# A decoder layer with routed experts: sends in fours, last additions on VectorE, longer runs in DRAM

## The chip, the cores and the metric

The kernel runs on one core of one Trainium2 chip. The core has five engines with instruction queues of their own: TensorE (PE, with its weight loads shown as PEld), VectorE (DVE), ScalarE (ACT), GpSimd (POOL) and SyncE (SP), and 16 DMA engines that they share. The metric is the device time of one execution in microseconds (us), as a median over runs. A separate execution is recorded by the hardware profiler, and all rows below come from that one.

## The reference

One pre-norm decoder layer in fp32 over 1024 tokens of width D = 256 (16 sequences of 64):

```python
x = x + attention(layernorm(x))          # 16 heads of 128, weights = codes * scales
x = x + cross_attention(layernorm(x), ctx)   # 16 heads, rope, low-rank keys and values
x = x + experts(layernorm(x))

def experts(x):
    scores = softmax(x @ Wg.T)                         # 16 experts in 4 groups
    # the 2 best groups, then the 4 best experts within them
    h = silu(x @ W1[e].T) * (x @ W3[e].T)              # inner width 176
    y = sum over the token's 4 experts of scores[e] * (h @ W2[e].T)
    z = (silu(x @ Ws1.T) * (x @ Ws3.T)) @ Ws2.T        # shared expert
    return y + z
```

## The kernel before, in words

Matrix products run on pairs of fp32r numbers: `parts_of` (L111) splits a value into a high part, written by ACT (L112), and a low part, written by DVE (L113), and `three` (L107) and `matmuls` (L104) multiply high by high, high by low and low by high. The tokens are held as eight tiles `x[i]` of 128 rows, in two halves of four tiles.

The cross attention goes through its 16 heads in quads of four. `quad_steps` (L403) loads a quad's weights from DRAM: `Wq` and `Wo` as 128 partitions with four pieces of 1024 bytes each, `w_kc_q` with four of 768, `w_kc_kv` with four of 256.

The experts follow. For each half, `choose` works out a target row for every token and each of its four choices k. `send` (L837) scatters the token's row, 272 floats or 1088 bytes, by indirect DMAs from POOL's queue into the DRAM buffer `xd`: 16 sends in each half, four for each k. Every expert but the last has 384 slots in `xd`. The last expert, and the tokens for which an expert's slots don't suffice, are computed densely. Then the loop over `e` takes the experts through a pipeline of stages:

- `expert_inputs(e)` (L1251) loads the expert's slots `xr` (408 KB, L1255, on SP's queue, behind the sends of choices 0 to e), PE transposes them in six pieces (L1265), ACT and DVE split them into `xs`.
- `expert_weights(e)` loads the raw weights `w` (640 KB, L277, on SP's queue, into one of two buffers) and splits them: ACT copies (L278), DVE and DVE or POOL subtract (L283).
- `expert_hidden` multiplies 18 times, ACT applies Silu in two steps (L1283, L1286), DVE multiplies (L1284, L1287), and the result is split into `hp`.
- `send_outputs` (L1291) multiplies by the second weights, copies the results to `y` (L1299, on ACT, one of three on DVE) and scatters them by three indirect DMAs from POOL's queue (L1304) to the rows of `yd` that belong to a token and its choice.

The loop computes the hidden layer of expert e-1 ahead of the slots of expert e where e is 1 or 2, and behind them otherwise:

```python
for e in range(E + 1):
    if e in (1, 2):
        hs[e - 1] = expert_hidden(ws[e - 1], xs[e - 1][0], SLOTS)
    ...
    if 0 <= e - 1 < E - 1 and e > 2:
        hs[e - 1] = expert_hidden(ws[e - 1], xs[e - 1][0], SLOTS)
```

After experts 11 to 14, `load_outputs(k)` (L1314) loads the outputs of one choice for all tokens, in four loads of 256 KB on SP's queue (L1320) into a pool of nine `got` buffers, each behind all sends of outputs that it may read. At the end `add_outputs` (L1327) adds each output, times the token's weight for it, to `x`. For two of three tiles that is one DVE instruction (L1334), for the third a scaling on ACT (L1331) and an addition on POOL (L1332). The dense part of the last expert for the second half lies between: `dense_hidden`, and `dense_output`, whose results `add_last` adds on DVE (L952). Eight DMAs store `x` (L1392), on the queues of SP and ACT in turn.

The order of instructions on each engine is fixed when the program is built: a scheduler works on estimated times of each instruction, and `issue_after` pins some of them behind others. A change of the program's text can thus move instructions that it doesn't name. Waits on semaphores are derived from buffers and from dependencies that the program declares; `side_by_side` declares that two sends do not depend on each other, and `behind` declares that a load depends on a list of sends.

Of the kernel before, what the change touches and what calls it, by code (L numbers as in the profile page):

```python
# [71 lines left out]
def decoder_layer(ctx: ExitStack, tc: tile.TileContext, a: dict, out: bass.AP):  # L72
# [167 lines left out]

    yd = dram.tile([(E - 1) * SLOTS + TOPK * NT, D], F32, tag="yd", name="yd")

    def side_by_side(sent, others):

        for other in others:
            tc.declare_no_dep(sent, other, reason="each writes rows of its own")
        others.append(sent)

    def behind(read, writes):
# [65 lines left out]
    with ExitStack() as attn:  # L315
# [87 lines left out]
        def quad_steps(qd, weights, pool):  # L403


            hs = slice(4 * qd, 4 * qd + 4)
            wq = raw_tile("wq", [128, 4, D])
            nc.sync.dma_start(
                out=wq,
                in_=a["Wq"][512 * qd : 512 * qd + 512, :].rearrange("(h k) d -> k h d", k=128),  # L410
            )
            wkq = raw_tile("wkq", [128, 4, DCQ])
            nc.sync.dma_start(out=wkq, in_=a["w_kc_q"][hs].rearrange("h k q -> k h q"))
            wqr = raw_tile("wqr", [R, 4, DCQ])
            nc.sync.dma_start(out=wqr, in_=a["W_qrT"][:, hs, :])
            wkr = raw_tile("wkr", [R, 4, DC])
            nc.sync.dma_start(out=wkr, in_=a["W_krT"][:, hs, :])
            wkv = raw_tile("wkv", [128, 4, DC])
            nc.sync.dma_start(out=wkv, in_=a["w_kc_kv"][hs].rearrange("h k d -> k h d"))
            wot = raw_tile("wot", [128, 4, D])  # L420
            quad_loads.append(
                nc.sync.dma_start(
                    out=wot,
                    in_=a["Wo"][512 * qd : 512 * qd + 512, :].rearrange(
                        "(h k) o -> k h o", k=128
                    ),
                ).ins
            )
            w_s = pool.tile([128, 3, 2, 2, DC], F32, tag="w_s", name="w_s")
            nc.gpsimd.memset(w_s, 0.0)  # L430
            yield
            w_q = [
                pool.tile([128, 2, 2, 4 * HQ], F32R, tag=f"w_q{n}", name=f"w_q{n}")
                for n in range(2)
            ]
            for h in range(4):
                ps = mm_tile(cols=2 * DCQ)
                for c in range(2):
                    nc.tensor.matmul(  # L439
                        ps[:, c * DCQ : (c + 1) * DCQ],  # L440
                        lhsT=wq[:, h, c * 128 : (c + 1) * 128],
                        rhs=wkq[:, h, :],
                        start=True,
                        stop=True,
                    )
                cols = slice(h * HQ, (h + 1) * HQ)
                parts_of(
                    ps.rearrange("p (c t j) -> p c t j", c=2, t=2),
                    w_q[0][:, :, :, cols],
                    w_q[1][:, :, :, cols],  # L450
                )
                if h % 2 == 1:
                    yield
            for tiles in ((0, 1), (2,)):
                ps = mm_tile().rearrange("p (t b n d) -> p t b n d", t=2, b=2, n=2)
                for t, row, n, blk, h, j in PIECES:
                    if t not in tiles:
                        continue
                    rows = slice(row, row + n)
                    for ab in range(2):  # L460
                        nc.tensor.matmul(  # L461
                            ps[rows, t % 2, blk, ab, :],
                            lhsT=wqr[:, h, ab * HQ + j : ab * HQ + j + n],
                            rhs=wkr[:, h, :],
                            start=True,
                            stop=True,
                        )
                for t, row, n, blk, h, j in PIECES:
                    if t in tiles:
# [15 lines left out]
            parts_of(ps, w_o[0], w_o[1])  # L485
            weights[qd].append(w_o)
            yield
# [348 lines left out]

        def send(half, choices=range(TOPK), waits=()):  # L837

            to = targets[half]
            for k in choices:  # L840
                for i in range(4):
                    sent = nc.gpsimd.indirect_dma_start(
                        out=xd[: TOPK * NT + (E - 1 - k) * SLOTS],
                        out_offset=bass.IndirectOffsetOnAxis(ap=to[:, k, i : i + 1], axis=0),
                        in_=rows[half][i // 2][:, i % 2, :],
                        in_offset=None,
                    ).ins
                    side_by_side(sent, sent_rows)
                    sent_for[k].append(sent)
                    behind(sent, waits)  # L850

# [399 lines left out]
    def expert_inputs(e):  # L1251

        t = fx.tile([128, SLOTS // 128, ROW], F32, tag="xr", name="xr", bufs=3)
        first = TOPK * NT + (E - 2 - e) * SLOTS
        load = nc.sync.dma_start(  # L1255
            out=t, in_=xd[first : first + SLOTS].rearrange("(b p) d -> p b d", p=128)
        ).ins
        for k in range(min(TOPK, e + 1)):
            behind(load, sent_for[k])
        to = fx.tile([128, SLOTS // 128], U32, tag="to", name="to", bufs=8)  # L1260
        parts = [fx.tile([128, 2, SLOTS], F32R, tag=f"xs{n}", name=f"xs{n}") for n in range(2)]
        for c in range(2):
            ps = at_tile([128, 512])[:, :SLOTS]
            for b in range(SLOTS // 128):
                nc.tensor.transpose(  # L1265
                    ps[:, b * 128 : (b + 1) * 128], t[:, b, c * 128 : (c + 1) * 128], ident
                )
            lows.append(parts_of(ps, parts[0][:, c, :], parts[1][:, c, :]))
        with tc.issue_after(lows[-1]):
            nc.vector.tensor_copy(to, t[:, :, D + e])  # L1270
        return parts, to
# [41 lines left out]

    def load_outputs(k):  # L1314

        tiles = []
        for n in range(NI // 2):
            t = fy.tile([128, 2, D], F32, tag="got", name="got", bufs=9)
            first = (E - 1) * SLOTS + (TOPK - 1 - k) * NT + n * 256
            got = nc.sync.dma_start(  # L1320
                out=t, in_=yd[first : first + 256].rearrange("(i p) d -> p i d", p=128)
            ).ins
            behind(got, returned)
            tiles.append(t)
        return tiles

    def add_outputs(k, got, cw):  # L1327
        for i in range(NI):
            y, w = got[i // 2][:, i % 2], cw[i // 4][:, k, i % 4 : i % 4 + 1]
            if i % 3 == 2:  # L1330
                nc.scalar.activation(y, y, AF.Copy, scale=w)  # L1331
                nc.gpsimd.tensor_tensor(x[i], x[i], y, ALU.add)  # L1332
            else:
                nc.vector.scalar_tensor_tensor(x[i], y, w, x[i], ALU.mult, ALU.add)  # L1334

    def dense_hidden(w, half, n):
        return expert_hidden(w, [p[:, :, n * 256 : n * 256 + 256] for p in normed[half]], 256)
# [13 lines left out]
    with tc.issue_after(lows[-1]), tc.issue_after(silus[-1]):  # L1351
        ws[0] = expert_weights(a["W123"][0], nc.vector)
    for e in range(E + 1):
        if e in (1, 2):

            low = lows[-1]
            hs[e - 1] = expert_hidden(ws[e - 1], xs[e - 1][0], SLOTS)
        if e < E - 1:
            low = lows[-1]
            with tc.issue_after(up_done[0] if e in (1, 2) else low):  # L1360
                xs[e] = expert_inputs(e)
            if e >= 1:
                with tc.issue_after(low), tc.issue_after(silus[-1]):
# [1 line left out]
        if e == 1:  # L1365
            with tc.issue_after(gated[0]), tc.issue_after(silus[-1]):
                routed.append(weights_of_choices(1))
        if 0 <= e - 1 < E - 1 and e > 2:
            hs[e - 1] = expert_hidden(ws[e - 1], xs[e - 1][0], SLOTS)
        if e - 2 >= 0:  # L1370
            if e == E:
# [9 lines left out]
    with ExitStack() as behind_last:  # L1381
        for ins in (*last, gated[0]):
            behind_last.enter_context(tc.issue_after(ins))
        cw = [r[0] for r in routed]
        add_outputs(0, got[0], cw)
        dense_output(w_last, h_p, 1, 0, add_last)
        add_outputs(1, got[1], cw)
        dense_output(w_last, dense_hidden(w_last, 1, 1), 1, 1, add_last)
        for k in range(2, TOPK):
            add_outputs(k, got[k], cw)  # L1390
    for i in range(NI):
        (nc.sync if i % 2 == 0 else nc.scalar).dma_start(  # L1392
# [123 lines left out]
```

## Time and profile before

| | |
|---|---|
| median of three runs | 570.32 us (569.85 to 570.35) |
| profiled execution | 577.4 us |
| its span | 575.5 us |
| mean granted PE clock | 0.978 of full speed |
| DMA | 70.83 MB in 56294 packets |
| entry into the experts | first slots loaded from 446.5 us on |
| last outputs stored | from 566.8 us on |

The profiled execution is 7.1 us above the median of the three runs. The busy shares of the page are averages over the span; the stages have different limits, so a stretch is read from its own windows and its own part of the timeline. In a timeline row the columns are the start, the duration, the engine, the line and operation, output and inputs, and in brackets the idle time before and what ended it. Several like instructions in a row are one line with a count.

### The profile page before, as it was taken

The page shows a single profiled execution, that of the slowest core. Times are in us where ns is not written, and L with a number is a line of the kernel's source. Part 1 is how long each engine was busy: PE and PEld are TensorE (multiplying, and loading weights), DVE is VectorE, ACT ScalarE, POOL GpSimd, SP SyncE. Part 2 cuts the span into 40 slices and gives each one's busy share as a digit, 9 for nine tenths or more (in the row PEclk, how much of TensorE's full clock was granted, in tenths as well). Part 3 has the DMA queues.
Part 4 walks back from the last instruction along what each step waited for, and adds up shares of the span by engine and source line. Part 5 has one row for each costly group of instructions (what it writes and reads, how often), then busy time and mean ns, then how long its engine had stood idle before and what let it go on. Part 6 is the DMA issues. An engine that isn't in the chain of part 4 may idle for free.

```text
span 575.5 us, 10603 instructions
## 1 busy us (share of the span) xinstructions
PE 540.3 (94%) x4013; PEld 446.7 (78%) x4013; DVE 400.2 (70%) x879; ACT 279.3 (49%) x524; POOL 230.6 (40%) x213
## 2 busy tenths in 40 slices
PE   7999999999999989999999999999999779999962
PEld 5889898888989876757778577685787669999951
DVE  6355566644655788848577586889777479999866
ACT  4677557575574431230432323152525187777551
POOL 4260500101001005426243444632544717888862
PEclk9999999999999999999999999999999789999995
DMA  8564431823200599482020000000511658777384
GB/s 227 145 166 146 111 109 39 227 86 112 75 1 1 167 250 308 111 239 52 2 70 1 8 1 1 0 31 0 188 50 68 202 169 285 240 245 238 122 279 152
DMA packets 56294, 70.83 MB, mean 123 GB/s; under 512 B 13872, under 2 KB 42768, under 8 KB 56240
## 3 DMA queue, kind: packets, MB, share of 16 engines
q1 hardware_dynamic: 51408, 58.71, 34.5%
q0 software_dynamic: 3696, 10.36, 4.7%
q10 hardware_dynamic: 1136, 1.05, 0.6%
q8 instruction: 33, 0.54, 0.4%
q14 instruction: 21, 0.17, 0.1%
HBM read 48.61 MB, written 21.86 MB: 122 GB/s over the span
## 4 chain that ended last, share of the span: by engine, by line
PE 81%; DVE 7%; issue 4%; DMA 3%; ACT 3%; POOL 1%; SPq 1%; DVEq 0%; ACTq 0%; POOLq 0%
PE mm L104 47%; PE mm L1005 7%; PE av L590 5%; PE av L104 5%; PE at L573 4%; PE at L343 3%; PE at L1028 2%; PE av L1041 2%; PE at L1265 2%; PE mm L439 2%; DMA bqkv<-in_bqkv 1%; PE mm L461 1%; DMA got<-yd 1%; DVE x L1334 1%; POOL roped L990 1%
## 5 line engine op out<-in xcount | busy, mean ns | idle before, releaser
L990 POOL TENSOR_TENSOR roped<-rt,rt 128x512 f32<-128x512 f32 x48 | 62.6, 1325 | 83.4 <-DVE rt L984 80.5
L984 DVE TENSOR_TENSOR rt<-mm,rope_q 128x512 f32<-128x512 f32 x96 | 61.4, 685 | 24.3 <-PE mm L104 23.6
L104 PE MATMUL mm<-xn,w_q 128*128 128x512 f32 x288 | 73.9, 403 | 0.5 <-ACT xn L222 0.5
L104 PEld LDWEIGHTS mm<-xn,w_q 128*128 128x128 f32 x288 | 52.2, 188 | 14.0 <-issue 1.8
L104 PE MATMUL mm<-xs,w 128*128 128x384 f32 x270 | 55.3, 354 | 7.0 <-ACT xs L112 5.8
L1304 POOL DMA_INDIRECT yd<-y,to x45 | 47.9, 1064 | 27.6 <-ACT y L1299 13.1
L104 PEld LDWEIGHTS mm<-xs,w 128*128 128x128 f32 x270 | 48.4, 198 | 9.0 <-ACT xs L112 6.6
L327 ACT ACTIVATE p<-p 128x512 f32<-128x512 f32 x32 | 20.1, 629 | 62.3 <-DVE p L326 62.3
L324 DVE TENSOR_REDUCE sm_m<-at 128x8 f32<-128x512 f32 x32 | 21.8, 680 | 37.1 <-PE at L573 36.2
L1005 PE MATMUL mm<-roped,w_s 128*64 128x512 f32 x192 | 46.4, 602 | 0.7 <-POOL roped L990 0.7
L522 POOL TENSOR_TENSOR wv<-code,scale 128x512 fp32r<-128x512 f32 x7 | 9.5, 1360 | 88.2 <-DMA scale<-in_scales 58.7
L613 DVE TENSOR_TENSOR x<-mm,x 128x256 f32<-128x256 f32 x64 | 26.0, 419 | 23.9 <-PE mm L104 21.9
L104 PE MATMUL mm<-wo,o 128*128 128x256 f32 x256 | 39.6, 295 | 0.0
L104 PE MATMUL av<-w,hp 128*128 128x256 f32 x225 | 35.2, 290 | 0.7 <-ACT y L1299 0.7
L104 PE MATMUL mm<-xn,wq 128*128 128x512 f32 x128 | 34.6, 405 | 0.7 <-ACT xn L222 0.5
L104 PE MATMUL mm<-wv,xn 128*128 128x256 f32 x256 | 35.2, 289 | 0.0
L104 PE MATMUL mm<-xn,wk 128*128 128x512 f32 x128 | 34.9, 404 | 0.0
L590 PE MATMUL av<-pt,v 128*128 128x128 f32 x256 | 34.5, 277 | 0.0
L104 PEld LDWEIGHTS mm<-wo,o 128*128 128x128 f32 x256 | 32.9, 190 | 1.5 <-issue 0.4
L590 PEld LDWEIGHTS av<-pt,v 128*128 128x128 f32 x256 | 32.0, 191 | 1.2
L104 PEld LDWEIGHTS mm<-wv,xn 128*128 128x128 f32 x256 | 31.8, 189 | 0.9
L104 PEld LDWEIGHTS av<-w,hp 128*128 128x128 f32 x225 | 30.6, 190 | 1.9 <-ACT y L1299 1.2
(216 smaller groups left out, 1145.8 us busy)
## 6 DMA issues: line engine op xcount, KB each, us to landing
w<-in_W SPq DMA_DIRECT2D x15, 640.0 KB
code<-in_codes SPq DMA_DIRECT2D x32, 256.0 KB
scale<-in_scales SPq DMA_DIRECT2D x32, 256.0 KB
xr<-xd SPq DMA_DIRECT2D x15, 408.0 KB
xd<-zeros SPq DMA_DIRECT2D x8, 720.0 KB
yd<-zeros SPq DMA_DIRECT2D x8, 512.0 KB
got<-yd SPq DMA_DIRECT2D x16, 256.0 KB
wq<-in_Wq SPq DMA_DIRECT2D x4, 512.0 KB
```

The lines of the kernel that those rows point to most:

```text
L104: m = nc.tensor.matmul(ps, lhsT=l, rhs=r, start=(n == 0), stop=(n == len(pairs) - 1))
L324: nc.vector.tensor_reduce(m, sc, AX.X, ALU.max)
L327: exps.append(nc.scalar.activation(p, p, AF.Exp, scale=scale).ins)
L343: last = nc.tensor.transpose(ps[:, 2 * n : 2 * n + 2, :].rearrange("p a q -> p (a q)"), pn[:, 2 * n : 2 * n + 2, :].rearrange("p a k -> p ...
L439: nc.tensor.matmul(ps[:, c * DCQ : (c + 1) * DCQ], lhsT=wq[:, h, c * 128 : (c + 1) * 128], rhs=wkq[:, h, :], start=True, stop=True,)
L573: nc.tensor.matmul(sc[par * 64 : par * 64 + 64, 2 * g + pp, :], lhsT=qk[0][:, b * S : (b + 1) * S], rhs=qk[1][:, b * S : (b + 1) * S], sta ...
L590: nc.tensor.matmul(av[:, k * 128 : (k + 1) * 128], lhsT=v[:, i, k0 : k0 + HD], rhs=pt[:, i].rearrange("p a q -> p (a q)"), start=True, sto ...
L613: nc.vector.tensor_tensor(x[i], ps, x[i], ALU.add)
L984: nc.vector.tensor_tensor(mt, ps3, rope_table(t, 2 * ab + k), ALU.mult)
L990: nc.gpsimd.tensor_tensor(r.rearrange("p (b s) -> p b s", s=S), one, two, op)
L1005: nc.tensor.matmul(ps[h // 2][(h % 2) * 64 : (h % 2) * 64 + 64], lhsT=w_s[:, t, blk, ab, :], rhs=roped[2 * t + ab], start=first[h], stop=l ...
L1304: sent = nc.gpsimd.indirect_dma_start(out=yd[: (E - 1) * SLOTS + min(TOPK, E - 1 - e) * NT], out_offset=bass.IndirectOffsetOnAxis(ap=to[:, ...
```

## The change

Seven things are changed.

1. In `send`, for the second half, the four sends of choices 1, 2 and 3 each wait until the last send before them has landed.
2. The slots `xr` are loaded with a partition's three rows side by side in DRAM (3264 bytes in one run, before three of 1088).
3. `load_outputs` takes two rows of `yd` side by side for a partition (2048 bytes, before two of 1024), and `row_of`, by which the outputs are scattered, is permuted to match. For the last choice the four tiles lie in the two raw-weight buffers, and two of the loads go to ACT's queue.
4. `add_outputs` makes all 32 additions on DVE.
5. At the end, the first dense output of the last expert comes ahead of the additions of choice 0, the second hidden layer and output ahead of the additions of choice 1.
6. At e = 3 too, the hidden layer of the expert before comes ahead of the slots.
7. The weights of the cross attention lie in DRAM by quads, so that a partition's piece is one run of 4096, 3072, 1024 and 4096 bytes.

In the built program, the order of instructions on every engine is the same up to the entry into the experts. There, SP's loads stand as xr 0, W 2, xr 1, xr 2, W 3, xr 3, where they stood as xr 0, xr 1, W 2, xr 2, xr 3, W 3.

```diff
-    def side_by_side(sent, others):
+    def side_by_side(sent, others, landed=()):
         for other in others:
-            tc.declare_no_dep(sent, other, reason="each writes rows of its own")
+            if other not in landed:
+                tc.declare_no_dep(sent, other, reason="each writes rows of its own")
         others.append(sent)
...
             wq = raw_tile("wq", [128, 4, D])
-            nc.sync.dma_start(
-                out=wq,
-                in_=a["Wq"][512 * qd : 512 * qd + 512, :].rearrange("(h k) d -> k h d", k=128),
-            )
+            nc.sync.dma_start(out=wq, in_=a["Wq"][qd])
...
             for k in choices:
+                landed = sent_rows[-1:] if half and k else ()
                 for i in range(4):
...
-                    side_by_side(sent, sent_rows)
+                    side_by_side(sent, sent_rows, landed)
...
-            out=t, in_=xd[first : first + SLOTS].rearrange("(b p) d -> p b d", p=128)
+            out=t, in_=xd[first : first + SLOTS].rearrange("(p b) d -> p b d", p=128)
...
-        tiles = []
-        for n in range(NI // 2):
-            t = fy.tile([128, 2, D], F32, tag="got", name="got", bufs=9)
+        if k == TOPK - 1:
+            tiles = [
+                t[:, n * 2 * D : (n + 1) * 2 * D].rearrange("p (i d) -> p i d", i=2)
+                for t in (fw.tile([128, W_COLS], F32, tag="w123", name="got_last") for _ in range(2))
+                for n in range(2)
+            ]
+        else:
+            tiles = [
+                fy.tile([128, 2, D], F32, tag="got", name="got", bufs=9) for _ in range(NI // 2)
+            ]
+        for n, t in enumerate(tiles):
             first = (E - 1) * SLOTS + (TOPK - 1 - k) * NT + n * 256
-            got = nc.sync.dma_start(
-                out=t, in_=yd[first : first + 256].rearrange("(i p) d -> p i d", p=128)
+            got = (nc.scalar if k == TOPK - 1 and n % 2 else nc.sync).dma_start(
+                out=t, in_=yd[first : first + 256].rearrange("(p i) d -> p i d", p=128)
             ).ins
...
-            if i % 3 == 2:
-                nc.scalar.activation(y, y, AF.Copy, scale=w)
-                nc.gpsimd.tensor_tensor(x[i], x[i], y, ALU.add)
-            else:
-                nc.vector.scalar_tensor_tensor(x[i], y, w, x[i], ALU.mult, ALU.add)
+            nc.vector.scalar_tensor_tensor(x[i], y, w, x[i], ALU.mult, ALU.add)
...
-        if e in (1, 2):
+        if e in (1, 2, 3):
...
-            with tc.issue_after(up_done[0] if e in (1, 2) else low):
+            with tc.issue_after(up_done[0] if e in (1, 2, 3) else low):
...
-        if 0 <= e - 1 < E - 1 and e > 2:
+        if 0 <= e - 1 < E - 1 and e > 3:
...
+        dense_output(w_last, h_p, 1, 0, add_last)
         add_outputs(0, got[0], cw)
-        dense_output(w_last, h_p, 1, 0, add_last)
-        add_outputs(1, got[1], cw)
         dense_output(w_last, dense_hidden(w_last, 1, 1), 1, 1, add_last)
-        for k in range(2, TOPK):
+        for k in range(1, TOPK):
             add_outputs(k, got[k], cw)
...
+    def quads(w):
+        return w.reshape(NQ, NH // NQ, HD, -1).transpose(0, 2, 1, 3)
+
+    arrays["Wq"] = quads(v[xa + "Wq"])
...
-    arrays["row_of"] = (
-        (E - 1) * SLOTS + TOPK * NT + np.arange(NT).reshape(NI, 128).T
-    ).astype(np.float32)
+    pairs = np.arange(NT).reshape(NI // 2, 128, 2).transpose(1, 0, 2).reshape(128, NI)
+    arrays["row_of"] = ((E - 1) * SLOTS + TOPK * NT + pairs).astype(np.float32)
```

More of the change, by code (lines that the diff above doesn't have):

```diff
@@ L407, in quad_steps @@
             wq = raw_tile("wq", [128, 4, D])
-            nc.sync.dma_start(
-                out=wq,
-                in_=a["Wq"][512 * qd : 512 * qd + 512, :].rearrange("(h k) d -> k h d", k=128),
-            )
+            nc.sync.dma_start(out=wq, in_=a["Wq"][qd])
             wkq = raw_tile("wkq", [128, 4, DCQ])
-            nc.sync.dma_start(out=wkq, in_=a["w_kc_q"][hs].rearrange("h k q -> k h q"))
+            nc.sync.dma_start(out=wkq, in_=a["w_kc_q"][qd])
             wqr = raw_tile("wqr", [R, 4, DCQ])
@@ L418, in quad_steps @@
             wkv = raw_tile("wkv", [128, 4, DC])
-            nc.sync.dma_start(out=wkv, in_=a["w_kc_kv"][hs].rearrange("h k d -> k h d"))
+            nc.sync.dma_start(out=wkv, in_=a["w_kc_kv"][qd])
             wot = raw_tile("wot", [128, 4, D])
             quad_loads.append(
[L422 to L427, printed above, removed]
+                nc.sync.dma_start(out=wot, in_=a["Wo"][qd]).ins
             )
@@ L1314, in load_outputs @@
     def load_outputs(k):
-        tiles = []
-        for n in range(NI // 2):
-            t = fy.tile([128, 2, D], F32, tag="got", name="got", bufs=9)
+        if k == TOPK - 1:
[9 more added lines that the diff above has]
+        for n, t in enumerate(tiles):
             first = (E - 1) * SLOTS + (TOPK - 1 - k) * NT + n * 256
-            got = nc.sync.dma_start(
-                out=t, in_=yd[first : first + 256].rearrange("(i p) d -> p i d", p=128)
+            got = (nc.scalar if k == TOPK - 1 and n % 2 else nc.sync).dma_start(
+                out=t, in_=yd[first : first + 256].rearrange("(p i) d -> p i d", p=128)
             ).ins
             behind(got, returned)
-            tiles.append(t)
         return tiles
@@ L1468 @@
     arrays["bo"] = v[sa + "bo"]
-    arrays["Wq"] = v[xa + "Wq"]
-    arrays["w_kc_q"] = v[xa + "w_kc_q"]
-    arrays["w_kc_kv"] = v[xa + "w_kc_kv"]
+    def quads(w):
+        return w.reshape(NQ, NH // NQ, HD, -1).transpose(0, 2, 1, 3)
+    arrays["Wq"] = quads(v[xa + "Wq"])
+    arrays["w_kc_q"] = quads(v[xa + "w_kc_q"])
+    arrays["w_kc_kv"] = quads(v[xa + "w_kc_kv"])
     arrays["W_qrT"] = v[xa + "W_qr"].transpose(2, 0, 1)
     arrays["W_krT"] = v[xa + "W_kr"].transpose(2, 0, 1)
-    arrays["Wo"] = v[xa + "Wo"].T
+    arrays["Wo"] = quads(v[xa + "Wo"].T)
     arrays["W123"] = _expert_weights(*(v[ff + n] for n in ("W1", "W3", "W2")))
```

## The prediction

> **What bounds the kernel now.** I read the page first, then the waits of PE, then PE's windows and timeline around the entry into the experts, and last the timeline of the end.
>
> ```profile
> PE 540.3 (94%) x4013; PEld 446.7 (78%) x4013; DVE 400.2 (70%) x879; ACT 279.3 (49%) x524; POOL 230.6 (40%) x213
> ...
> PE 81%; DVE 7%; issue 4%; DMA 3%; ACT 3%; POOL 1%; SPq 1%; DVEq 0%; ACTq 0%; POOLq 0%
> ```
>
> PE is busy for 94% of the 575.5-us span, and 81% of the chain that ended last is PE. A change gains only where PE waits, or in the last stretch, where PE has run out of work. What PE waits for:
>
> ```profile
> PE av L104 <- DVE x L952: 5.8, 2, 4.2
> PE mm L104 <- ACT xs L112: 5.8, 3, 3.2
> ```
>
> These two are the largest of 21 lines (total, times, longest), and none of the 21 names a DMA. The first lies in the last 15 us. The second is the entry into the experts. PE's timeline there, with idle time and releaser in brackets:
>
> ```profile
> 450.68 1.13 PE L104 MATMUL mm<-ws,sh 96*128 96x256 f32 x4 [1.65 <-issue]
> ...
> 454.54 4.82 PE L104 MATMUL mm<-xs,w 128*128 128x384 f32 x18 [1.45 <-ACT xs L112]
> 459.19 0.82 PE L1265 MATMUL at<-ident,xr 128*128 128x128 f32 x6
> 463.24 0.79 PE L104 MATMUL mm<-xs,w 128*128 128x384 f32 x3 [3.23 <-ACT xs L112]
> ...
> 471.41 0.80 PE L104 MATMUL mm<-xs,w 128*128 128x384 f32 x3 [1.10 <-ACT xs L112]
> 472.48 1.08 PE L104 MATMUL av<-w,hp 128*128 128x256 f32 x7 [0.27 <-ACT y L1299]
> 473.56 0.55 PE L1265 MATMUL at<-ident,xr 128*128 128x128 f32 x3
> ```
>
> PE waits at 463.24 and at 471.41 for experts 1 and 2, the two where the loop computes the previous hidden layer ahead of the transposes. From expert 3 (transposes at 473.56 and 475.64) it waits no more. The windows (width, then busy time of PE, PEld, DVE, ACT, POOL, granted clock, DMA share, GB/s):
>
> ```profile
> 450.00:452.00 2.00, 1.32 (x6) 1.32 (x7) 2.00 (x4) 0.00 (x0) 1.85 (x1) 0.70 0.23 81
> 452.00:454.00 2.00, 1.09 (x6) 0.69 (x4) 1.71 (x6) 0.00 (x0) 1.39 (x3) 0.50 0.43 122
> ...
> 480.00:490.00 10.00, 10.00 (x74) 10.00 (x73) 9.18 (x17) 8.40 (x18) 6.63 (x7) 1.00 0.83 277
> 490.00:500.00 10.00, 9.97 (x69) 9.77 (x68) 9.09 (x18) 6.96 (x17) 7.93 (x7) 1.00 0.66 214
> ```
>
> From 472.5 to 550 PE is full (10.00 or 9.63 of 10). Time lost at expert 3 is therefore lost at the end.
>
> The end, from the timeline, is a chain of additions by DVE:
>
> ```profile
> 552.59 3.65 DVE L1334 SCALAR_TENSOR_TENSOR x<-got,cw,x 128x256 f32<-128x256 f32 x9
> 557.09 2.08 POOL L1332 TENSOR_TENSOR x<-x,got 128x256 f32<-128x256 f32 x3
> 558.62 0.85 DVE L1334 SCALAR_TENSOR_TENSOR x<-got,cw,x 128x256 f32<-128x256 f32 x1 [2.38 <-DMA got<-yd]
> ...
> 566.12 0.51 ACT L1331 ACTIVATE got<-got,cw 128x256 f32<-128x256 f32 x1 [1.00 <-DMA got<-yd]
> ...
> 569.50 1.66 DVE L1334 SCALAR_TENSOR_TENSOR x<-got,cw,x 128x256 f32<-128x256 f32 x4
> ```
>
> DVE starts the additions at 552.59 and ends at 571.16. The outputs are then stored and the span ends at 575.5.
>
> **The change part by part.** The sum is made against the profiled execution: 577.4 us, of which 575.5 are the span. It lies 7.1 us above the median of the three runs (570.32), and I carry differences over to the median unchanged.
>
> *Weights of the cross attention as quads.* Sixteen loads (L408 to L427) keep place and bytes and get longer runs. No line of PE's waits names a DMA and nobody is listed as waiting for wq: 0. If that cover went, a shorter load would still not be later. Both bounds are near 0.
>
> *Loop order at e = 3.* Hidden layer 2 (18 matmuls, about 3.4 us at full clock) moves ahead of the transposes of xr 3. The instruction order of the two kernels shows PE then runs as at e = 2: hidden matmuls, six transposes, output matmuls, hidden matmuls of the next expert. ACT's order becomes two Silus, the raw-weight copy of L278, first xs part, hp, second xs part, y. So the row for e = 2 is the price, and it is 1.10 + 0.27 us of idle plus about 0.25 between the pieces, 1.6. Built up by hand: hidden 2 has 15 matmuls left at 473.56, 0.19 each, and ends at 476.4, transposes at 477.2, seven output matmuls at 478.05. ACT ends its second Silu at 477.1, its 1.26-us copy at 478.4 and the first xs part at 478.9: PE waits 0.9. Three matmuls take it to 479.5. The next output matmuls wait for y, behind hp 0.5, xs 0.5 and y 0.37, until 480.35: 0.8. Together 1.7. The bounds are 0 (the copy comes early enough and PE finds other work in its queue) and 2.2 (DVE's 0.96-us L283 gets ahead of the xs parts). Nothing below 0, because before has no wait there. Each 10-us window behind it has at most 0.37 us of idle, so hardly any is made good. Taken: +1.7.
>
> *The clock behind that gap.* In the rows above, 1.65 us of idle ended at 450.68 and the granted clock fell to 0.70 and then 0.50; the 18 matmuls at 454.54 took 4.82 us there instead of 3.4. The Trainium skill, "TensorE: Matmul & The Clock Gate", section "HAM oscillation — how this bites in real kernels", asks that PE have no idle gap over about 3.4 us; by that rule gaps of 0.9 and 0.8 cost nothing and the sum for this part is +1.7. By the trace a gap of half that length can be followed by half clock, and one more hidden layer at half clock costs 1.4: +3.1. The gap at 471.41 (1.10) was followed by 1.00, and it is the nearer in size. I weigh 1.4 by somewhat under one half: +0.6.
>
> *Sends in fours.* Three waits are added on POOL (before k = 1, 2 and 3 of half 1), each for the landing of the last send of the four before. Queued behind each are only later sends, until the first send of outputs at 472.70, before which POOL already sits idle for 11.50 us. A send takes 0.96 us at a pitch of 1.27 and the wait for its landing is bounded by xr 0, which waits for the first four sends: it leaves at 446.53, 2.0 behind the fourth send's end at 444.52. Three gates cost up to 2.0 each, 6 us for k = 3, which would end by 467 instead of 461.2. Who waits is the loads of xr 1, 2 and 3 on SP. On SP, W2 and W3 also change places with xr 1 and xr 3: W2 ahead of xr 1 (it waits for DVE's L283 until 452.1, so xr 1 leaves near 452.9 instead of 452.36 and shares the engines with 640 KB), xr 3 ahead of W3. xr 1 landing 1.5 later than its 455.7 is still ahead of its transposes at 459.19. xr 2 leaves near 460, as now (459.83), for transposes at 469.02. xr 3 leaves by 469 instead of 463.50 and lands by 472.5, for transposes that the new loop order puts at 476.5. W3 lands behind it, by 475, for a copy at 477.1. The bounds are +2 (each gate twice as dear) and -0.5 (xr loads that no longer share with sends): taken 0.
>
> *xr in runs of 3264 bytes.* 408 KB in longer runs is a few tenths of a us, on loads with 2 to 6 us of slack: 0.
>
> *The end.* Removed are 8 scalings on ACT (L1331, 0.507 each) and 8 additions on POOL (L1332, 0.733); added are 8 additions on DVE. Nine of those took 3.65 us in a row, 0.41 each, so DVE gets 3.3 more. What DVE no longer suffers: L1334 has 470 / 480 / 1021 ns (minimum, median, maximum) over 24 and a mean of 576 in the end, so 24 x 0.096 = 2.3 are slow instances, and one hp part took 0.97 instead of 0.42, with POOL's additions running beside all of them: 2.9. The Trainium skill, "SBUF — State Buffer", section "SBUF: two separate sides", has DVE and GpSimd share a pair of ports as an exclusive lock held for a whole instruction. By it the eight POOL additions (5.9 us busy) could block for up to 5.9, and taking them away would gain 2.6 net. By the trace the loss is 2.9, and the net is +0.4. I take the trace.
>
> Then the work ahead of DVE from 552.59 is 32 x 0.41 + 4 additions of the dense expert at 0.41 + four parts of the hidden layer at 0.43 = 16.5, so 569.1 if it never waits, against 571.16. It waits for loads: the third choice near 559 (+0.8), the last choice near 563.4 (+0.4). The last choice's four loads now go into the raw-weight buffers, consumed by 544, and leave from two queues once the sends have landed, near 561. Before, they left one by one up to 562.46, and the last landed near 566.1 to 566.8 (the ACT wait at 566.12). Loads n = 1 and 3 sit on ACT's queue ahead of its last hp part, which waits for the sends too; the dense output behind it is off DVE's list until it comes, and DVE has choices 1 and 2 to add meanwhile. DVE's end: 570.3, a gain of 0.85. The bounds: -2.1 (no waits), and +1.3 (if loads are quick when no profiler runs, before would lose its wait of 2.38 and end earlier, while after is held by DVE's own 16.5). Between them I take -0.5. Moving the dense output ahead of the first additions fills PE's idle and is inside this figure. Runs of 2048 bytes for these loads are too.
>
> Sum: 0 + 1.7 + 0.6 + 0 + 0 - 0.5 = +1.8: 579.2 for the profiled execution, 572.1 for the median.
>
> **The rivals.**
> (a) Faster, by one mechanism: the end becomes DVE's own work. Without POOL additions beside it and with the last choice's loads freed onto two queues, DVE ends 1.5 to 2.1 earlier, near 569.1 to 569.6, while the wait at expert 3 comes to 0.4 or less, because xr 3 and W3 arrive early enough for ACT to copy before the second Silu. It decides when the end gains more than expert 3 loses. For it speaks that DVE has no wait after 558.62 now; against it that ACT's order at e = 3 repeats that of e = 2, which waited. Time: 570.3 - 1.7 + 0.3 = 568.9.
> (b) The gap halves the clock: +1.7 + 1.4 and 0.6 more while it recovers, less 0.5: 573.5.
> (c) The gates make slots late: xr 3 or W3 beyond 477 instead of by 475. Then PE stands 2 to 4 us: 574 to 576. Against it: 2 to 4 us of slack.
> (d) The change does less than it says: the wait at 471.41 belongs to that place alone and the end is tied: 570.5.
>
> **How the numbers follow.** The main case (571.4 to 573) has 0.45, (a) 0.18, (b) 0.15, (c) 0.07, (d) 0.15. A measurement of this kernel tells 0.2% from no change, 1.14 us: same is 569.18 to 571.46. Slower is most of the main case (0.38), (b) and (c): 0.60. Same is 0.07 of the main case and 0.11 of (d): 0.18. Faster is (a) and the rest of (d): 0.22. The range leaves out the worse half of (c), the far end of (b) and the best of (a): 568.4 to 575.2. The main case alone is 571.2 to 573.2.
>
> **What would show it.** Right: PE's timeline has a wait for ACT xs L112 of about 0.9 and one for y of about 0.8 between 477 and 481, and PE is full behind it; the clock there reads 1.00 or falls; the transposes of xr 3 wait for no DMA; L1332 is gone, L1334 counts 32 near 480 ns without the 1021; the last loads leave together and DVE ends near 570.3 plus what came before. Wrong: no wait at expert 3 (then the order wasn't the cause), DVE's end earlier by over 1.5 relative to 552.59, a PE wait for DMA, or a difference ahead of 446 us, where only the runs of weight loads changed.

## The result and the profile after

The changed kernel takes 572.75 us (median of five runs, 571.68 to 574.6), the kernel before 569.85 (five runs) beside it: a ratio of 1.0055, 95% interval 1.0041 to 1.0069. It is slower by 2.9 us. The profiled execution of the changed kernel took 571.68 us, with a span of 569.8.

The profile of before that the prediction was read from took 577.4 us, though the median beside the changed kernel is 569.85. It is no fair partner for the profile after. So the kernel before was profiled once more (label b_again below, 569.34 us, span 567.5), and the comparisons here are with that second profile unless they say otherwise. Its PE reaches the entry into the experts about 2 us earlier than in the first profile, and leaves it about 8 us earlier (DVE's first addition of an output is at 544.39 instead of 552.59).

The page of the changed kernel, parts 1 and 4:

```profile
PE 536.5 (94%) x4013; PEld 443.2 (78%) x4013; DVE 402.7 (71%) x887; ACT 275.7 (48%) x516; POOL 223.4 (39%) x205
...
PE 83%; DVE 8%; ACT 3%; DMA 2%; issue 2%; POOL 1%; SPq 0%; DVEq 0%; ACTq 0%; POOLq 0%
```

The waits of PE in the changed kernel (total, times, longest):

```profile
PE at L1261 <- DMA xr<-xd: 4.1, 3, 2.3
PE av L104 <- DVE hp L113: 3.3, 2, 2.0
...
PE mm L104 <- ACT xs L112: 0.4, 2, 0.2
```

The largest is one that the first profile of before does not have at all: PE's transposes wait for the slots to land. The wait for ACT's xs is down to 0.4. PE's timeline of the changed kernel at the entry, with idle time and releaser in brackets:

```profile
455.10 0.85 PE L1261 MATMUL at<-ident,xr 128*128 128x128 f32 x6 [2.29 <-DMA xr<-xd]
...
457.69 2.88 PE L104 MATMUL mm<-xs,w 128*128 128x384 f32 x9
...
462.58 0.84 PE L1261 MATMUL at<-ident,xr 128*128 128x128 f32 x6 [0.73 <-DMA xr<-xd]
...
465.15 1.08 PE L104 MATMUL av<-w,hp 128*128 128x256 f32 x7 [0.27 <-ACT y L1295]
...
470.30 0.84 PE L1261 MATMUL at<-ident,xr 128*128 128x128 f32 x6 [1.07 <-DMA xr<-xd]
...
471.79 0.69 PE L104 MATMUL mm<-xs,w 128*128 128x384 f32 x3
```

The three rows of L1261 are the transposes of xr 1, 2 and 3. The same stretch in the second profile of before:

```profile
453.69 0.85 PE L1265 MATMUL at<-ident,xr 128*128 128x128 f32 x6 [0.71 <-DMA xr<-xd]
455.22 0.79 PE L104 MATMUL mm<-xs,w 128*128 128x384 f32 x3 [0.68 <-ACT xs L112]
...
457.02 1.83 PE L104 MATMUL mm<-xs,w 128*128 128x384 f32 x9 [0.55 <-DVE xs L113]
...
459.99 0.84 PE L1265 MATMUL at<-ident,xr 128*128 128x128 f32 x6
...
463.39 0.80 PE L104 MATMUL mm<-xs,w 128*128 128x384 f32 x3 [2.09 <-ACT xs L112]
464.45 1.08 PE L104 MATMUL av<-w,hp 128*128 128x256 f32 x7 [0.27 <-ACT y L1299]
```

Before, PE waited 0.71 us for xr 1 and never for xr 2 or 3; its large wait (2.09, at expert 2) was for ACT. At the seven output matmuls behind that place the changed kernel is 0.70 late (465.15 against 464.45); its wait of 1.07 for xr 3 follows. Nine matmuls of the hidden layer took 1.83 us before and 2.88 in the changed kernel. The windows of the changed kernel show why (the granted clock is the third number from the end):

```profile
456.00:458.00 2.00, 1.81 (x8) 1.81 (x9) 1.94 (x6) 1.98 (x5) 1.39 (x2) 0.70 0.19 70
458.00:460.00 2.00, 2.00 (x8) 2.00 (x8) 1.79 (x10) 1.60 (x3) 0.57 (x1) 0.50 0.19 70
```

The end of the changed kernel, DVE's timeline:

```profile
546.32 3.65 DVE L1333 SCALAR_TENSOR_TENSOR x<-got,cw,x 128x256 f32<-128x256 f32 x9
...
553.70 0.88 DVE L1333 SCALAR_TENSOR_TENSOR x<-got,cw,x 128x256 f32<-128x256 f32 x2 [1.51 <-DMA got<-yd]
...
558.47 1.67 DVE L1333 SCALAR_TENSOR_TENSOR x<-got_last,cw,x 128x256 f32<-128x256 f32 x4 [1.01 <-DMA got_last<-yd]
...
564.41 0.88 DVE L1333 SCALAR_TENSOR_TENSOR x<-got_last,cw,x 128x256 f32<-128x256 f32 x2
```

and of before, second profile:

```profile
544.39 3.65 DVE L1334 SCALAR_TENSOR_TENSOR x<-got,cw,x 128x256 f32<-128x256 f32 x9
...
550.76 0.60 DVE L1334 SCALAR_TENSOR_TENSOR x<-got,cw,x 128x256 f32<-128x256 f32 x1 [2.72 <-DMA got<-yd]
...
561.14 1.66 DVE L1334 SCALAR_TENSOR_TENSOR x<-got,cw,x 128x256 f32<-128x256 f32 x4
```

Two readings of these timelines serve throughout. DVE's first addition of an output (546.32 against 544.39) tells how late PE comes out of the experts, +1.93. The time from there to the end of the last addition (to 565.29, and to 562.80) is the end: 18.97 us against 18.41. In this execution, the fastest of the five, most of the loss is in the entry; the experiments show that the end can cost as much.

### The profile page after: what moved, and what is told of

Read it like the earlier page. It is cut to its first block, busy times and chain, and to the rows that moved or that the text cites. A ratio compares the mean times of both kernels' runs of the same rounds, so it can differ in the third digit from the quotient of the medians.

```text
span 569.8 us, 10586 instructions
## 1 busy us (share of the span) xinstructions
PE 536.5 (94%) x4013; PEld 443.2 (78%) x4013; DVE 402.7 (71%) x887; ACT 275.7 (48%) x516; POOL 223.4 (39%) x205
## 4 chain that ended last, share of the span: by engine, by line
PE 83%; DVE 8%; ACT 3%; DMA 2%; issue 2%; POOL 1%; SPq 0%; DVEq 0%; ACTq 0%; POOLq 0%
PE mm L104 50%; PE mm L1001 7%; PE av L104 5%; PE av L584 5%; PE at L567 4%; PE at L345 3%; PE at L1024 2%; PE av L1037 2%; PE mm L433 2%; DVE x L1333 1%; ACT w L280 1%; PE at L1261 1%; PE mm L455 1%; DMA got_last<-yd 1%; POOL roped L986 1%
## 5 line engine op out<-in xcount | busy, mean ns | idle before, releaser
L104 PEld LDWEIGHTS mm<-xs,w 128*128 128x128 f32 x270 | 46.9, 193 | 5.4 <-ACT w L280 2.4
```

The source lines that it names most:

```text
L104: m = nc.tensor.matmul(ps, lhsT=l, rhs=r, start=(n == 0), stop=(n == len(pairs) - 1))
```

## The experiments

**A second profile of before (b_again).** No edit.

> The kernel before, unchanged, for a second profiled execution. The one shown before took 577.4 us against a median of 569.85, and its PE was level with the changed kernel's until the matmul number 3100 of 4013 (405.6 us) and lost 7.0 us to it by number 3400. If that was a loss of this one execution (theory: the clock at 0.50 between 452 and 458, after idle gaps), this profile ends 5 to 7 us earlier, shows a granted clock near 1.00 through the entry into the experts, no PE wait for the DMA of xr, and about 569.5 to 570.5 us. Rival: the first profile is typical for the stage and the changed kernel really gains 5 us there and loses it elsewhere; then this profile again shows 3.2 us of PE idle for expert 1 and a clock of 0.50.

Measured: 569.34 us, span 567.5, a granted clock of 1.00 in every 2-us window from 440 to 468, and 1.1 us in all of waiting for xr, where none was expected. The first profile is not typical of the executions that the result compares, as the theory had it. That it was a loss of that one execution is not shown: the profiles from other chips, below, look like it. What follows is uncomfortable for the prediction: all its figures of slack at the entry were read where PE arrived up to 8 us late.

**The changed kernel without the waits of sends (a_no_gate).** These waits, each for the landing of the four sends before, are called gates from here on.

```diff
-                landed = sent_rows[-1:] if half and k else ()
+                landed = ()
```

> The changed kernel without the waits of sends for the landing of the group before; all else kept. SP's loads then stand with xr 1 ahead of W 2 again. Theory 1 (the gates make the slots late; PE waits 2.3, 0.7 and 1.1 us for the DMA of xr 1, 2 and 3 in the changed kernel's profile): those three waits go, and the time falls by 2.5 to 4 to 569 to 570.3. Rival, theory 2 (the loop order at e = 3 is what costs, about 1.7, and the gates are hidden): no PE wait for xr disappears without another taking its place, the time stays at 572 to 573.

Measured: 573.41 us, 1.0056 (1.0042 to 1.0070). The time did not fall, so theory 1 fell as stated. The waits for xr 2 and xr 3 went (0.5 us is left, for xr 0 and 1), and at expert 3 stands what the prediction had expected there (the last two rows). The first row is an earlier hidden layer, slow as in the changed kernel:

```profile
456.75 2.79 PE L104 MATMUL mm<-xs,w 128*128 128x384 f32 x9 [0.56 <-DVE xs L113]
...
471.07 0.79 PE L104 MATMUL mm<-xs,w 128*128 128x384 f32 x3 [0.82 <-ACT xs L112]
472.14 0.86 PE L104 MATMUL av<-w,hp 128*128 128x256 f32 x5 [0.27 <-ACT y L1295]
```

The window of this run shows the clock at 0.50 there, although the largest gap of PE ahead of it at the entry is 1.12 us (the granted clock is again the third number from the end):

```profile
458.00:460.00 2.00, 2.00 (x8) 2.00 (x8) 1.62 (x10) 1.15 (x2) 0.20 (x1) 0.50 0.77 294
```

DVE's first addition is at 546.34, as late as with the gates. Its end took 20.72 us, 1.75 more than in the changed kernel's profile, with the same instructions:

```profile
554.46 0.88 DVE L1333 SCALAR_TENSOR_TENSOR x<-got,cw,x 128x256 f32<-128x256 f32 x2 [2.26 <-DMA got<-yd]
...
560.24 1.67 DVE L1333 SCALAR_TENSOR_TENSOR x<-got_last,cw,x 128x256 f32<-128x256 f32 x4 [2.02 <-DMA got_last<-yd]
```

**The changed kernel with the loop order of before (a_no_e3).**

```diff
-        if e in (1, 2, 3):
+        if e in (1, 2):
...
-            with tc.issue_after(up_done[0] if e in (1, 2, 3) else low):
+            with tc.issue_after(up_done[0] if e in (1, 2) else low):
...
-        if 0 <= e - 1 < E - 1 and e > 3:
+        if 0 <= e - 1 < E - 1 and e > 2:
```

> The changed kernel with the loop order of before at e = 3 (hidden layer 2 behind the slots of expert 3), all else kept, the gates too. Theory 2 (the order costs 1.7): 571. Theory 1 (the gates cost, and the order hides part of it): xr 3 lands near 470 in the changed kernel, and the transposes of xr 3 now stand about 4 us earlier in PE's order, so PE waits about 4 us there: 574 to 577.

Measured: 578.58 us, 1.0146 (1.0126 to 1.0166), 5.8 above the changed kernel. DVE's first addition is at 551.45. PE's timeline of this run at the transposes of xr 3:

```profile
471.26 0.87 PE L1261 MATMUL at<-ident,xr 128*128 128x128 f32 x3 [3.67 <-DMA xr<-xd]
471.78 3.23 PE L104 MATMUL mm<-xs,w 128*128 128x384 f32 x9
```

With the gates, the loop order at e = 3 is not a cost but what hides them: the hidden layer ahead of the transposes fills 3 us in which xr 3 is still on its way. The time lies above the 574 to 577 expected of theory 1; nine matmuls behind the wait take 3.23 us, where the nine of the rows above took 1.83 at full clock.

Together with the second profile of before (which has neither edit, and not the layouts or the new end) this makes a table of DVE's first addition, in us behind 544.39, from one profile each:

| | order of before | hidden layer first at e = 3 |
|---|---|---|
| no gates | 0 | 1.95 |
| gates | 7.06 | 1.93 |

The two edits do not add up. With the new order the gates cost nothing more (1.95 and 1.93, by different waits), and with the gates the new order saves 5.13.

**The changed kernel with the end of before (a_old_tail).**

```diff
-        if k == TOPK - 1:
-            tiles = [... the raw-weight buffers ...]
-        else:
...
-            got = (nc.scalar if k == TOPK - 1 and n % 2 else nc.sync).dma_start(
+            got = nc.sync.dma_start(
...
+            if i % 3 == 2:
+                nc.scalar.activation(y, y, AF.Copy, scale=w)
+                nc.gpsimd.tensor_tensor(x[i], x[i], y, ALU.add)
+            else:
...
-        dense_output(w_last, h_p, 1, 0, add_last)
         add_outputs(0, got[0], cw)
+        dense_output(w_last, h_p, 1, 0, add_last)
+        add_outputs(1, got[1], cw)
...
-        for k in range(1, TOPK):
+        for k in range(2, TOPK):
```

> The changed kernel with the end of before: outputs of the last choice in the pool of nine, all loads on SP's queue, every third addition on ACT and POOL, and the dense outputs behind the additions of choices 0 and 1. The runs of 2048 bytes are kept. In the two profiles DVE needs 18.57 us from its first addition to its last before and 18.97 after. If the new end brings nothing (what the profiles say): the time stays within 0.8 of the changed kernel's 572.75. If it gains the 0.5 of the prediction or more: 573.2 to 574.5. If it costs: below 572.

Measured: 571.07 us, 1.0027 (1.0018 to 1.0035), in 12 runs. The interval lies wholly below that of the changed kernel, so the new end costs: 572.75 - 571.07 = 1.7 us. The remaining 1.2 of the loss belong to the gates, the order and the layouts together; no run beside the result takes the layouts alone. In its profile the first addition is at 546.70 and the end takes 18.06 us. Which of the parts of the new end costs was not taken apart.

**Kernels on other chips.** The remaining runs fell on two other chips, on which the kernel before itself takes 577.07 and 577.21 us. Their times are read only against the kernel before beside them, and the profiles against the first profile of before, which is like them: PE's matmul number 3300 of 4013 starts at 439.57 in it, at 439.46 to 439.96 in six of the eight profiles from these chips (later in the other two), and at 437.06 to 437.34 in the second profile of before and in the changed kernel and its variants above. The 18 runs of before beside those variants lie between 568.58 and 571.65. So the first profile shows what these chips do. On which chip it was taken is not on record.

The changed kernel without gates and with the order of before (a_entry_old, both edits from above):

> The changed kernel without the waits of sends and with the loop order of before at e = 3: left of the change are the layouts and the new end. Theory (either of the two edits at the entry costs about 2 us, and they don't add up because each hides the other; the new end costs 0.4 to 2.2): PE's matmul number 3900 is back at the time of the kernel before (533.5 us in its second profile, against 535.25 changed), and the time is 570.3 to 571.8. Rival (the 2 us at the entry come from the layouts, slots with 3264-byte runs or permuted rows, not from gates and order): number 3900 stays near 535, and the time near 572.5.

Measured: 1.0008 (0.9959 to 1.0058): it tells nothing. Repeated as a_entry_old_2:

> The changed kernel without the waits of sends and with the loop order of before at e = 3, once more, since the runs of it scattered by over 2%. Theory: entry as before, the changed kernel's end with 0.5 to 2.2 us more than before's: 1.001 to 1.004. Rival (the layouts cost at the entry): 1.005 or more.

Measured: 577.61 us, 1.0001 (0.9985 to 1.0017), below the 1.001 to 1.004 expected. DVE's end took 18.13 us in its profile, against 18.57 in the first profile of before.

The layouts alone in the kernel before (layouts, and repeated as layouts_2): the edits of `quad_steps`, of `expert_inputs`, and of the runs and rows in `load_outputs`.

> The kernel before with the layouts alone: weights by quads, slots in runs of 3264 bytes, outputs in runs of 2048 bytes with the permuted rows. Theory (loads are hidden or short of nothing): within 0.6 of the kernel before, 569.3 to 570.5. Rival (the longer runs shorten the loads that the entry and the end wait for): 568 to 569.2. Second rival (the rows of a slot tile stand in another order, and the layouts cost at the entry): above 571.

> The kernel before with the layouts alone, once more for the same reason. Theory: 0.999 to 1.001. Rival (longer runs bring the loads of slots and outputs earlier): 0.996 to 0.998. In the first run of it DVE's end took 16.6 us without a wait, on executions in which it began 9.6 us later than in the kernel before's second profile; if the runs of 2048 bytes do that, the end is again under 17.2 here; if it was the late start that let the loads land first, it is 18.0 to 18.4.

Measured: 1.0007 (0.9958 to 1.0056), then 576.51 us, 0.9983 (0.9963 to 1.0003). On these chips a cost of them is not shown; by layouts_2 it is under 0.2 us. A gain of up to 2 us is not excluded and not shown. The end took 16.64 us in the first profile and 18.40 in the second, with the same program, so the short end was no work of the layouts. layouts_2 differs from a_entry_old_2 by the new end alone, on the same chip: 576.51 without it and 577.61 with it, with intervals that overlap. A cost of the new end is not shown on this chip, nor excluded.

**Additions in the order of the choices.** In the changed kernel DVE's list has, behind the two dense additions (L948), two additions of choice 2 ahead of four of choices 0 and 1 for the two tiles that the dense additions have just left. Those four need nothing but outputs whose loads were issued earlier; they stand behind an instruction that waits. A pin sets them ahead: `added` collects the additions as they are made, and those of a later choice are ordered behind them. It is in a_ordered for every choice and in a_pin2 for choices 2 and 3:

```diff
...
-            add_outputs(k, got[k], cw)
+            with ExitStack() as behind_choice:
+                for ins in added if k >= 2 else ():     # a_ordered: for ins in added[-NI:]
+                    behind_choice.enter_context(tc.issue_after(ins))
+                add_outputs(k, got[k], cw)
```

> The changed kernel, with the additions of a choice pinned behind those of the choice before on DVE, nothing else. Theory (in the changed kernel DVE has an addition of choice 2 ahead of seven of choices 0 and 1 that were ready, and waits 1.5 us for its load, then 1.0 for the last choice's; in two variants 2.3 and 2.0, 2.6 and 1.6): the first wait goes, DVE needs about 17 to 18 us from first to last addition instead of 19.0 to 20.7, and the time falls by 1 to 2.5, to 570.3 to 571.7. Rival (the end is set by when the last choice's loads land, whatever comes before): DVE waits as long, only later, and the time stays at 572 to 573.

> The changed kernel with the additions of choices 2 and 3 pinned behind those of choices 0 and 1 on DVE; the order is otherwise that of the changed kernel. Theory (an addition of choice 2 stands ahead of seven that are ready): DVE has no wait for got of 1.5 to 2.6 us, its end takes 16.7 to 17.5 us from first to last addition where the changed kernel took 19.0 to 20.7, and the time is 1.5 to 3 below the changed kernel's, at 1.000 (0.998 to 1.003) of the kernel before. Rival (the landing of the last loads sets the end): no change beyond noise, 1.004 to 1.006.

Measured: a_ordered 574.88 us, 0.9948 (0.9904 to 0.9992); a_pin2 575.56 us, 0.9977 (0.9964 to 0.9989), in 22 runs. The end of a_pin2 in DVE's timeline:

```profile
549.16 3.71 DVE L1334 SCALAR_TENSOR_TENSOR x<-got,cw,x 128x256 f32<-128x256 f32 x9
553.74 0.42 DVE L1280 TENSOR_TENSOR h<-mm,g 128x256 f32<-128x256 f32 x1 [0.88 <-ACT g L1279]
...
559.18 0.91 DVE L948 SCALAR_TENSOR_TENSOR x<-av,cl,x 128x256 f32<-128x256 f32 x2 [0.89 <-PE av L104]
560.01 4.04 DVE L1334 SCALAR_TENSOR_TENSOR x<-got,cw,x 128x256 f32<-128x256 f32 x10
563.96 3.25 DVE L1334 SCALAR_TENSOR_TENSOR x<-got_last,cw,x 128x256 f32<-128x256 f32 x8
```

No wait for a DMA is left; 18 additions run in one go, at 0.40 us each, and those of the last choice find their loads landed. So the rival, that the landing of the last loads sets the end, falls. But the end takes 18.05 us (17.91 in a_ordered), where 16.7 to 17.5 were expected of a_pin2: 1.77 are waits for the second hidden layer and output of the dense expert. a_entry_old_2, without the pin, took 18.13 on the same chip. That the pin gains 1.5 to 3 us over the changed kernel was not shown in time, since the changed kernel itself was not run on that chip.

**The pins, without gates and with the order of before (best, best2).**

> The layouts and the new end with additions in the order of the choices, without the waits of sends and with the loop order of before at e = 3. Theory: entry as before, and an end that is 0.5 to 1.5 shorter than the 18.4 us of the kernel before: 568.4 to 569.6. Rival (DVE's own 16.5 us plus loads is no better than sharing with POOL and ACT): 570 to 571.

> As the run before this one, and without the waits of sends and with the loop order of before at e = 3. Theory: PE as in the kernel before up to the end, and an end of 16.7 to 17.5 us where before has 18.4: 0.997 to 0.999 of the kernel before. Rival (the entry's loss is not from those two edits): 1.000 to 1.003, as the run before this one.

Measured: 0.9993 (0.9950 to 1.0035), and 577.98 us, 1.0017 (1.0004 to 1.0031). The theory fell. best2 differs from a_entry_old_2 by the pin alone (577.98 with it, 577.61 without, the intervals overlap): here the pin is not shown to gain any time.

On this chip, taking the gates and the order away from a_pin2 costs 577.98 - 575.56 = 2.4 us; the intervals do not overlap. Beside the result the same two edits, with the layouts, stand for a loss of about 1.2. The profiles show the place. PE's timeline of layouts_2, which has neither edit, at the entry:

```profile
450.74 0.74 PE L104 MATMUL mm<-ws,sh 96*128 96x256 f32 x4 [1.65 <-issue]
453.85 6.10 PE L104 MATMUL mm<-xs,w 128*128 128x384 f32 x18 [1.71 <-ACT xs L112]
```

and of a_pin2, which has both:

```profile
449.94 0.87 PE L1261 MATMUL at<-ident,xr 128*128 128x128 f32 x6 [0.24 <-issue]
...
452.56 2.87 PE L104 MATMUL mm<-xs,w 128*128 128x384 f32 x15 [0.35 <-DVE xs L113]
```

Without gates PE stands for 1.65 us where nothing in the profile releases it, is late for xr 0, and runs most of the 18 matmuls of the first hidden layer at half clock (6.10 us; the granted clock is 0.50 to 0.55 from 454 to 460). The same 1.65 is in the first profile of before; no such wait is in the second profile or in a_no_gate, which have no gates either. With gates it is 0.24.

## Why the prediction was right, and where it was not

The forecast was 572.1 us, slower; measured were 572.75. The direction and the size hold, but the +2.9 is composed otherwise than the +1.8 of the sum: by a_old_tail about 1.2 at the entry and 1.7 at the end, where the sum had 2.3 and -0.5. By the prediction's own signs its account failed: PE waits for the DMA of the slots, and in the changed kernel it does not wait for ACT at expert 3. That the number came out is in good part luck.

*Weights as quads, 0.* Held. PE is level with before up to the entry: the profile of the changed kernel and the second of before differ by 0.17 us at 434, and the layouts alone measure 1.0007 and 0.9983, neither told from 1.

*Loop order, +1.7.* The mechanism was right, but it shows only without the gates: in a_no_gate PE waits 0.82 for ACT's xs and 0.27 for y (predicted 0.9 and 0.8), and comes out of the experts 1.95 late, of which only 0.26 are there ahead of expert 3 (464.71 against 464.45 at the seven output matmuls). In the changed kernel as it is, PE stands for xr 3 (1.07), and ACT is ready by then. The step that failed is that this term was costed apart from the gates; with the gates present the order saves 5.1 (551.45 against 546.32).

*The clock, +0.6.* A fall came, at another gap, and is not shown to have cost time. Behind the wait of 2.29 for xr 1 the clock falls to 0.70 and 0.50 and nine matmuls take 2.88 instead of 1.83. But PE's next wait, 0.73 for xr 2, ends when that load lands, and the load left SP's queue at 459.30, as the sends of choice 2 landed (POOL's next send waits for them until 459.43, below); at full clock the wait would have been longer by those 1.05 us (an estimate from these two rows). The length of one gap does not tell when the clock falls: the gap of 2.09 in the second profile of before, and those of 0.73 and 1.07, are followed by 1.00, and a_no_gate has the fall behind gaps of 1.12 us and less. By the rule of the Trainium skill ("TensorE: Matmul & The Clock Gate", "HAM oscillation — how this bites in real kernels") none of these gaps was long enough to cost; the measurement decides, and the clock fell in both runs. What decides it stays open.

*Sends in fours, 0.* Wrong. The size of the gates was right (up to 6 us for choice 3). POOL's timeline of the changed kernel, the first sends of choices 1, 2 and 3 and the last send, and then the last send of the second profile of before:

```profile
443.85 1.06 POOL L838 DMA_INDIRECT xd<-rows,to  x1 [1.73 <-DMA xd<-rows,to]
...
452.73 0.96 POOL L838 DMA_INDIRECT xd<-rows,to  x1 [3.51 <-DMA xd<-rows,to]
...
459.43 0.96 POOL L838 DMA_INDIRECT xd<-rows,to  x1 [1.73 <-DMA xd<-rows,to]
...
463.21 0.96 POOL L838 DMA_INDIRECT xd<-rows,to  x1 [0.30 <-issue]
```

```profile
457.51 0.96 POOL L842 DMA_INDIRECT xd<-rows,to  x1 [0.30 <-issue]
```

The last send ends at 464.17; before, it ended at 458.47, 5.7 earlier. The gate of 3.51 is the one during which W 2 loads, which now leaves SP's queue ahead of xr 1 (447.77); a_no_gate takes back both, so they are not told apart. What failed was the slack. The prediction had PE at the transposes of xr 1, 2 and 3 at 459.19, 469.02 and 476.5; in the second profile PE wants xr 1 before 453.69 and already waits 0.71 for it. Rival (c) was the mechanism, at 2 to 4 us and a chance of 0.07, with a slack of 2 to 4 us against it that the first profile shows and the second does not. The 4.1 us of waits cost less than that, since they stand where before waited for ACT (3.0 us).

*The end, -0.5.* Wrong in sign beside the result: +1.7 by the runs of a_old_tail. DVE's own work was sized rightly: the changed kernel's end less its two waits is 18.97 - 2.52 = 16.45 us, against 16.5. L1333 has no slow instance left (476 / 480 / 485 ns for minimum, median and maximum; the maximum is 1376 in a_old_tail, with POOL's additions back), which fits the lock that the prediction took from the Trainium skill ("SBUF — State Buffer", "SBUF: two separate sides"); no run here puts the sharing back alone. The mis-sized term is DVE's waits for loads: 0.8 + 0.4 predicted; 1.51 + 1.01, 2.26 + 2.02 and 2.63 + 1.61 in three profiles (the changed kernel, a_no_gate, a_no_e3), against 2.72 in the second profile of before and 1.93 in a_old_tail. The prediction said that DVE has other choices to add meanwhile. It has, but they stand behind in its list; a_pin2 and a_ordered show that the waits for loads go when they stand ahead. That time is gained by it is not shown.

Open is how the 2.9 us divide between runs of the changed kernel (571.68 to 574.6): its profile is the fastest of them, with the shortest of three ends.

## What to carry to other kernels

Before reading slack from a profile, set the profiled time against the median; if it stands out from the runs (here by 1.2%), take a second profile, since slack read where an engine comes late is too long. Two edits at one place, each with its own wait, must be costed together: here one hid the other, and taking away either alone gained nothing or cost 6 us. An engine whose list is fixed has ready work only if it stands ahead of the instruction that waits, so check the order of the list before writing that a wait is filled. And a wait that goes is not yet time gained: other waits came in its place.

## What the runs showed of the hardware that was not expected

The same program takes 569.9 us on one chip and 577.1 to 577.2 on two others, and the two profiles of before, one like each kind, are level within 0.5 us to 405 us. By PE's matmul number 3350 (447.00 and 444.77) the first is behind, with waits of PE for ACT and DVE, the largest 0.96 at 436.10; then come the 1.65 us at 450.68 that the profile calls issue, and half clock behind them. Half 1's sends are issued in a row at that time. An edit of the sends' timing together with the loop order has the opposite sign on these chips: about +1.2 us, layouts included, on the one, -2.4 on the other. Why the chips differ stays open.
